# Two graph layers on one core: layer 1's linear part in 16 bits, its roots on GpSimd, and the copies re-dealt

## The chip, the core and the metric

The kernel runs on one core of a Trainium2 chip. The core has a matrix engine (TensorE, PE in the profile; its weight loads are PEld), three engines for element-wise work (VectorE or DVE, ScalarE or ACT, GpSimd or POOL), and SyncE (SP), which here only issues transfers. Each engine runs its own instructions in the order in which they were written, and waits where an operand or a buffer is not ready. PE writes to PSUM[...]. The metric is the time of one execution on the device in microseconds (us). Of the kernel before there are three runs: 272.62, 273.17 and 273.79, so the median is 273.17 us.

## What is computed

There are 4096 nodes with 64 features each, and a 0/1 adjacency matrix of 4096 x 4096 whose ones are rare (one in 256). Cut to what matters:

```python
# layer 0
mask = (adj != 0)
rank = cumsum(mask, axis=1)
deg  = rank[:, -1:]
k    = minimum(deg, 100)
pos  = rank - (deg - k)
w    = mask * where(pos > 0, 0.5 ** (k - pos), 0)      # the last neighbour weighs 1, the one before 1/2, ...
x    = layernorm(x + (w @ (x @ W0) + b0))
# layer 1
h    = (adj @ x + x) / (deg + 1)
out  = relu(concat([x, h]) @ W1 + b1)
out  = out / maximum(norm(out, axis=1), 1e-12)
x    = layernorm(x + out)
```

Layer 1 needs all rows of layer 0's result before any of its rows is complete, but sums over the rows that exist can begin early.

## The kernel before

**Tiles and steps.** The 4096 output rows are eight slabs `g` of 512 rows (R). The neighbours are eight groups `k` of 512, each of four blocks of 128 (KB = 4). Tile (g, k) of the transposed adjacency is 128 partitions x 4 x 512; it is loaded by POOL's queue from float32 into bf16 (512 KB in SBUF). The main loop has 64 steps, one for each tile: slab after slab, `k` from 7 down to 0, because a neighbour's weight depends on how many neighbours come after it. Step `i` is tile `steps[i]`.

**A step.** `count` (L237) adds up, on PE, how many ones each half block has; DVE turns this into the running count `cs` (L247, L249). `spread` (L255) makes from it, on PE, the number of later neighbours for every half block (`rep`), and ACT makes `near` of it (L257). `weigh` (L270, L280) adds on PE the place within the half block and the part from `near`; ACT (L287) and DVE (L288) each turn half of that into the 16 bits of the weight (`w`). `gather` (L298) multiplies the previous step's `w` with x, held as two fp16 parts side by side (`xhl`: high, and low times 2048), into `acc0`.

**Chunks.** `count` and `spread` do not run for one tile but for a chunk of them, and one chunk ahead: while a chunk is weighed, the tiles of the next one are counted. Slab 0 has chunks of one tile, slabs 1 to 3 of two, slabs 4 to 7 of four. A chunk of two has both tiles of the next one counted in its first step.

**Layer 0's end of a slab** is spread over the following steps by `at(i, engine, function)`: with i = 8(g+1), `first_hT` (ACT copies `acc0`, at i+1), `first_pz` (PE, W0 and the degree), `first_y`, `first_mv` (DVE, i+2), `first_s` (ACT, square root, i+3), `first_r`, `first_x1` (DVE, i+4), `first_hi`, `first_xl`, `first_lo` (the two fp16 parts `x1hl` of the new x, i+5 and i+6). Then x's part of layer 1: `first_px` (i+5) transposes x on PE in float32, `first_x1T` copies it to SBUF (ACT, i+6), and `first_pu` (PE, i+6) multiplies it, with a row of ones for b1, with both halves of W1 in float32 (L447). `first_c1` (DVE) adds the two results.

**Layer 1's sums** start in the loop: `some_sums` does up to four matmuls a step (L307) on the tiles of rows whose layer 0 is done (`ready`), and `evict_part` keeps sums of a part of the rows in SBUF.

**Buffers.** There are 23 bf16 tiles. Layer 1 needs every tile again, so the tiles of slabs 0 to 3 with k from 4 to 7 are copied to fp8 (`keep_next`, L320, one half tile a step from step 8 on, on ACT: 32 copies of 128 x 1024), which frees the bf16 tile for a later load. POOL issues one load a step, and stops at a load whose buffer is still read.

**The tail** is written out by hand. `own` completes each slab's sums, `last_hT` brings them to SBUF, `last_pz` multiplies with W1's lower half, `last_z` adds `c1`, `last_sq` and `last_ss` sum the squares, and `root_a` (ACT's square root) with `root_b` (four DVE instructions, L370 to L374) gives one over the norm. `last_y` scales (DVE) and adds x (POOL); `last_mv` takes mean and variance; root_a and root_b give one over the deviation; `last_o` scales and shifts, and the result is stored. This goes by units: slabs 5 and 2, then 0 and 1, then 4 and 3, then 6, then the halves 7a and 7b, each with roots of its own. On DVE, `last_hT` of slab 6 stands behind `last_y` of unit 4 and 3.

```python
n = 1 if g == 0 else 2 if g < 4 else 4
at(i + 5, PE, first_px, g)
at(i + 6, ACT, first_x1T, g)
at(i + 6, PE, first_pu, g)
return i >= NK * (k + 1) + 6 and i >= when[g, k]
```

## Time and profile before

| what | value |
|---|---|
| median of three runs | 273.17 us (272.62 to 273.79) |
| the profiled execution | 273.33 us |
| its span, first to last instruction | 271.5 us |
| mean granted TensorE clock | 0.965 |
| PE busy | 237.3 us (87%), 1865 instructions |
| DVE busy | 176.3 us (65%), 480 instructions |
| ACT busy | 157.9 us (58%), 226 instructions |
| POOL busy | 61.9 us (23%), 111 instructions |
| read from HBM | 69.34 MB |

A line of a group or of a timeline reads: start and duration in us (in a timeline), the engine, the line of the kernel, the operation, what it writes <- what it reads, the shape, how often. What stands in brackets is the time that the engine sat idle before it, and what ended that. The slices divide the span in 40 equal parts; a digit is the busy share in tenths, 9 is 90% or more. Busy shares are averages over stages that have different limits, so each stage is read by itself. Matmul ends are modelled; the distance from one start to the next is the better measure.

### The profile page before, as it was taken

To read this page: it belongs to the slowest core of one execution; us is meant where nothing else is said; L and a number is where in the kernel's file an instruction comes from. 1 tells how busy PE (TensorE), PEld (TensorE's weight loads), DVE (VectorE), ACT (ScalarE), POOL (GpSimd) and SP (SyncE) were. 2 spreads that over 40 slices of the span, in tenths; PEclk is the share of its full clock that TensorE was granted. 3 is DMA by queue.
4 is the path that set the end of the run, shared out by engine and by line. 5 is a ranking of instruction groups with operands and counts; after the bars stand their busy time and mean duration, and the time that the engine had idled before them with its cause. 6 is when DMAs were issued, how large, how long until landed. Compare 5 with 4: busy or idle time off the path is not lost.

```text
span 271.5 us, 4838 instructions
## 1 busy us (share of the span) xinstructions
PE 237.3 (87%) x1865; PEld 105.0 (39%) x1865; DVE 176.3 (65%) x480; ACT 157.9 (58%) x226; POOL 61.9 (23%) x111
## 2 busy tenths in 40 slices
PE   8397688979899999999899999999998999997820
PEld 2122124334434343443344344434343546555710
DVE  5566634875596778367846684576577456597884
ACT  4456627897798869768854463436545322146351
POOL 8565551231101320322122121210200000221100
PEclk9979959999999999999999999999999999999985
DMA  6999999999997999799999999990500000010010
GB/s 97 195 230 234 241 212 214 222 214 214 223 214 141 165 211 214 124 171 214 182 179 205 203 162 180 168 168 12 98 2 0 0 2 0 0 42 20 19 58 21
DMA packets 12072, 37.13 MB, mean 137 GB/s; under 512 B 2066, under 2 KB 3218, under 8 KB 12050
## 3 DMA queue, kind: packets, MB, share of 16 engines
q0 software_dynamic: 10128, 35.66, 68.1%
q1 hardware_dynamic: 1922, 1.18, 1.5%
q8 instruction: 14, 0.23, 0.3%
q14 instruction: 8, 0.07, 0.1%
HBM read 69.34 MB, written 1.05 MB: 259 GB/s over the span
## 4 chain that ended last, share of the span: by engine, by line
PE 51%; DVE 11%; ACT 8%; issue 3%; POOL 1%; DVEq 0%; POOLq 0%; ACTq 0%
PE acc L298 10%; PE acc_part L307 9%; PE v L270 8%; PE v L280 5%; ACT w L287 4%; PE acc_right L307 3%; DVE w L288 3%; PE cnt L237 3%; PE vb L307 3%; PE pu L447 2%; PE va L307 2%; PE pz L594 2%; PE pz L395 2%; DVE x L422 1%; ACT a L320 1%
## 5 line engine op out<-in xcount | busy, mean ns | idle before, releaser
L288 DVE TENSOR_SCALAR w<-v 128x1024 int16<-128x1024 f32 x64 | 78.2, 1222 | 45.3 <-PE v L280 45.2
L287 ACT ACTIVATE w<-v,less 128x1024 int16<-128x1024 f32 x64 | 71.3, 1114 | 56.9 <-PE v L280 39.9
L298 PE MATMUL acc<-w,xhl 128*128 128x512 bf16 x256 | 67.2, 385 | 2.4 <-ACT hT L389 2.1
L109 POOL DMA_DIRECT2D a<-in_adjT_dram x65 | 35.5, 548 | 122.1 <-PE acc_part L307 49.9
L270 PE MATMUL v<-a,tri 64*64 64x512 bf16 x512 | 42.0, 397 | 4.3 <-ACT w L287 2.6
L298 PEld LDWEIGHTS <-xhl 128*128 128x128 f16 x256 | 23.9, 99 | 32.5 <-issue 9.5
L320 ACT CAST a<-a 128x1024 fp8e4<-128x1024 bf16 x32 | 33.3, 1039 | 0.0
L307 PEld LDWEIGHTS <-x1hl 128*128 128x128 f16 x224 | 19.8, 98 | 27.0 <-issue 5.7
L307 PE MATMUL acc_part<-a,x1hl 128*128 128x512 bf16 x108 | 28.0, 381 | 1.8 <-ACT x1hl L434 1.3
L247 DVE TENSOR_TENSOR cs<-cnt,cs 128x512 bf16<-128x512 f32 x20 | 13.8, 691 | 20.5 <-PE cnt L237 20.4
L237 PE MATMUL cnt<-a,pick 128*32 128x512 bf16 x256 | 21.9, 399 | 6.0 <-DMA a<-in_adjT_dram 6.0
L280 PE MATMUL v<-near,mine 32*128 32x512 bf16 x256 | 25.7, 391 | 0.2 <-ACT near L257 0.2
L270 PEld LDWEIGHTS <-tri 64*64 64x64 bf16 x512 | 12.6, 106 | 30.2 <-issue 28.0
L257 ACT ACTIVATE near<-rep,most 128x512 bf16<-128x512 f32 x28 | 19.1, 682 | 3.8 <-PE rep L255 3.7
L633 POOL TENSOR_TENSOR y<-y,x 128x256 f32<-128x256 f32 x7 | 5.0, 726 | 56.1 <-DVE y L630 56.1
L280 PEld LDWEIGHTS <-mine 32*128 32x128 bf16 x256 | 6.5, 91 | 24.9 <-issue 24.9
L255 PE MATMUL rep<-cs,further 128*128 128x512 bf16 x28 | 11.2, 400 | 3.7 <-DVE cs L247 1.7
L307 PE MATMUL acc_right<-a,x1hl 128*128 128x512 fp8e4 (+1 forms) x56 | 12.7, 379 | 0.0
L237 PEld LDWEIGHTS <-pick 128*32 128x32 bf16 x256 | 4.6, 94 | 19.8 <-issue 11.5
L655 ACT ACTIVATE o<-y,off,r_l 128x64 f32<-128x64 f32 x28 | 9.7, 428 | 3.1 <-issue 1.7
L382 DVE BATCH_NORM_STATS2 st_l<-y 128x6 f32<-128x64 f32 x60 | 9.0, 214 | 0.7 <-POOL y L633 0.6
L427 ACT CAST x1hl<-x 128x256 f16<-128x256 f32 x8 | 3.2, 406 | 10.1 <-DVE x L422 10.1
(139 smaller groups left out, 238.6 us busy)
## 6 DMA issues: line engine op xcount, KB each, us to landing
a<-in_adjT_dram POOLq DMA_DIRECT2D x63, 512.0 KB, 9.7
c<-in_x_pairs_dram POOLq DMA_DIRECT2D x8, 128.0 KB, 11.6
x<-in_x_dram POOLq DMA_DIRECT2D x8, 128.0 KB, 7.9
out_dram<-o SPq DMA_DIRECT2D x7, 128.0 KB, 1.7
a<-in_adjT_dram POOLq DMA_DIRECT2D x2, 256.0 KB, 4.7
out_dram<-o_7a SPq DMA_DIRECT2D x1, 64.0 KB, 1.9
out_dram<-o_7b SPq DMA_DIRECT2D x1, 64.0 KB, 1.5
w_sb<-in_L_gnn_weight_dram SPq DMA_DIRECT2D x2, 16.0 KB, 6.5
```

Of the source, the lines that this page charges most:

```text
L109: nc.gpsimd.dma_start(out=a[:, qs, :], in_=adjT[g, k][:, qs, :])
L237: nc.tensor.matmul(cnt[g][q * 32 : (q + 1) * 32, :], lhsT=pick[:, PW - 2 * k : PW - 2 * k + 32], rhs=A[g][k][:, q, :], start=first, stop=last,
L247: nc.vector.tensor_tensor(new, cnt[g], cs[g], ALU.add)
L255: nc.tensor.matmul(pr, lhsT=further, rhs=cs[g], start=True, stop=True)
L257: nc.scalar.activation(near[g], pr, AF.Relu, bias=most, scale=-1.0)
L270: nc.tensor.matmul(v[i][halves[c], r, :], lhsT=tri[halves[r], :], rhs=A[g][k][halves[r], 2 * i + c, :], start=True, stop=False,)
L280: nc.tensor.matmul(v[i][:, r, :], lhsT=mine[rows, 2 * k : 2 * k + 2, :], rhs=nr[rows, :], start=False, stop=True,)
L287: nc.scalar.activation(w[:, 0:2, :], v[0], AF.Relu, bias=less)
L288: nc.vector.tensor_scalar(w[:, 2:4, :], v[1], -STEP * MAX_NEIGH, 0.0, ALU.add, ALU.max)
L298: nc.tensor.matmul(acc0[g], lhsT=xhl[:, b, :], rhs=w[:, q, :].bitcast(BF16), start=(k, q) == (NK - 1, 0), stop=(k, q) == (0, KB - 1),)
L307: nc.tensor.matmul(acc, lhsT=x1hl[:, b, :], rhs=A[g][b // KB][:, b % KB, :], start=first, stop=last)
L320: nc.scalar.copy(kept[g, k][:, qs, :], A[g][k][:, qs, :], saturate=False)
```

## The change

Seven things change.

1. Chunks of slab 1: four of one tile, then two of two; slabs 2 and 3 stay at four of two, slabs 4 to 7 at two of four.
2. `first_px` transposes `x1hl`, both fp16 parts at once, in fp16; `first_x1T` copies 128 x 512 instead of 64 x 512; `first_pu` is twelve matmuls with W1 in three bf16 parts (`w1_parts`, upper 64 partitions scaled by 1/2048) and one with ones and b1 in three bf16 parts. All three, and `ready`, come one step later. The parts are made on DVE in steps 7 and 8; W1 comes in four pieces and b1 for all partitions.
3. ACT's Sqrt runs once at the start, on a constant.
4. The fp8 copies skip steps that begin a slab, and start at step 9; in every fourth step DVE does one instead of ACT: 23 for ACT, 9 for DVE. They end at step 44 instead of 39.
5. `first_hT` is written right after the slab's last `gather`, ahead of the next copies.
6. In the tail, `root_p` on POOL (x to the power -0.5) takes the place of root_a and root_b for all norms but 7b's, and for the deviations of units 5 and 2, 0 and 1, and 6. Their offsets are made on POOL in two instructions.
7. The tail's order: slab 6's `last_hT` ahead of `last_y` of unit 4 and 3, slab 6's `last_pz` after a quarter of 7a's sums, outputs in pieces; 7a and 7b keep norms of their own but share one root for the deviation, one `last_o` and one store. 7a's x is added on POOL.

The diff, cut:

```diff
-        n = 1 if g == 0 else 2 if g < 4 else 4
-        chunks += [[(g, k) for k in range(k0, k0 - n, -1)] for k0 in range(NK - 1, -1, -n)]
+        sizes = {0: [1] * 8, 1: [1] * 4 + [2] * 2, 2: [2] * 4, 3: [2] * 4}.get(g, [4] * 2)
+        k = NK
+        for n in sizes:
+            chunks.append([(g, k - 1 - i) for i in range(n)])
+            k -= n
...
+    nc.scalar.activation(zero, zero, AF.Sqrt)
...
-    x1T = const.tile([D + 1, R], F32, name="x1T")
-    nc.vector.memset(x1T[D : D + 1, :], 1.0)
+    power = const.tile([P, 2 * TB], F32, name="power")
+    nc.vector.memset(power, -0.5)
+    x1T = const.tile([P, R], FP16, name="x1T")
+    ident16 = const.tile([P, P], FP16, name="ident16")
+    nc.vector.tensor_copy(ident16, ident)
...
+        for h in range(2):
+            for c in range(2):
+                nc.sync.dma_start(out=w1_sb[h * D : (h + 1) * D, c * D : (c + 1) * D], in_=w1[c * D : (c + 1) * D, :])
+        nc.sync.dma_start(out=b1_sb, in_=b1.partition_broadcast(P))
...
     def prepare_last():
         nc.vector.tensor_scalar(wn_sb[D:P, :], wn_sb[D:P, :], 1.0 / LO, None, ALU.mult)
+        nc.vector.tensor_scalar(w1_sb[D:P, :], w1_sb[D:P, :], 1.0 / LO, None, ALU.mult)
+        for j in range(3):
+            nc.vector.tensor_copy(w1_parts[:, j, :], w1_sb)
+            if j < 2:
+                nc.vector.tensor_tensor(w1_sb, w1_sb, w1_parts[:, j, :], ALU.subtract)
...
-        nc.scalar.copy(kept[g, k][:, qs, :], A[g][k][:, qs, :], saturate=False)
+        if i % 4 == 3:
+            nc.vector.tensor_copy(kept[g, k][:, qs, :], A[g][k][:, qs, :], saturate=False)
+        else:
+            nc.scalar.copy(kept[g, k][:, qs, :], A[g][k][:, qs, :], saturate=False)
...
-        return i >= NK * (k + 1) + 6 and i >= when[g, k]
+        return i >= NK * (k + 1) + 7 and i >= when[g, k]
...
+    def root_p(v, eps, name, tag):
+
+        n = v.shape[1]
+        r = small.tile([P, n], F32, tag=tag, name=f"{tag}_{name}")
+        if eps:
+            nc.gpsimd.tensor_scalar(r, v, eps, None, ALU.add)
+            v = r
+        nc.gpsimd.tensor_tensor(r, v, power[:, 0:n], ALU.pow)
+        return r
...
-        px = ep["px", g] = ps_m.tile([D, R], F32, tag="m", name=f"px_{g}")
+        px = ep["px", g] = ps_m.tile([P, R], FP16, tag="m", name=f"px_{g}")
         for t in range(TB):
-            nc.tensor.transpose(px[:, ts(t, P)], x1[:, g * TB + t, :], ident)
+            nc.tensor.transpose(px[:, ts(t, P)], x1hl[:, g * TB + t, :], ident16)
...
         for t in range(TB):
-            nc.tensor.matmul(pu[:, t, :], lhsT=x1T[:, ts(t, P)], rhs=w1_sb, start=True, stop=True)
+            for j in range(3):
+                nc.tensor.matmul(
+                    pu[:, t, :], lhsT=x1T[:, ts(t, P)], rhs=w1_parts[:, j, :], start=(t, j) == (0, 0), stop=False
+                )
+        nc.tensor.matmul(pu[:, :, 0:D], lhsT=ones.to_broadcast([P, P]), rhs=b1_parts, start=False, stop=True)
...
-    at(2 * NK + 2, DVE, prepare_last)
+    at(NK - 1, DVE, prepare_last)
+    at(NK, DVE, prepare_b1)
...
-        at(i + 1, ACT, first_hT, g)
...
-        at(i + 5, PE, first_px, g)
-        at(i + 6, ACT, first_x1T, g)
-        at(i + 6, PE, first_pu, g)
+        at(i + 6, PE, first_px, g)
+        at(i + 7, ACT, first_x1T, g)
+        at(i + 7, PE, first_pu, g)
...
-            if i >= NK:
-                keep_next()
+            if i > NK and i % NK:
+                keep_next(i)
             if held is not None:
                 gather(*held)
             held = (g, k, w)
+            if g > 0 and k == NK - 1:
+                first_hT(g - 1)
...
+    def last_rn(u, on_pool):
+        name, bs = u
+        ss = ep["ss", name]
+        if on_pool:
+            ep["rn", name] = root_p(ss, None, name, "rn")
+        else:
+            ep["rn", name] = root_b(root_a(ss, zero, f"n_{name}"), ss, zero, f"n_{name}")
...
+    def last_r(u, on_pool):
+        name, bs = u
+        v = ep["mv1", name][:, :, 1]
+        if on_pool:
+            ep["r1", name] = root_p(v, LN_EPS, name, "r1")
+            offset(u, nc.gpsimd)
+        else:
+            ep["r1", name] = root_b(ep["s1", name], v, eps_ln, f"l1_{name}")
+            offset(u, nc.vector)
...
     last_ss(u)
...
-    last_rn(u)
-    last_y(u, True)
+    last_rn(u, True)
     last_hT(6)
     acc[L, 0] = acc_of(L, "acc0", R // 2, "7a")
-    own_half(a_half, 0, NB // 2)
-    last_mv(u)
+    own_half(a_half, 0, NB // 4)
 
     v = unit(6)
     last_pz(v)
-    own_half(a_half, NB // 2, NB)
-    last_r(u, True)
+    own_half(a_half, NB // 4, NB)
+    last_y(u, True)
     last_z(v)
     last_sq(v, False)
     last_ss(v)
+    last_rn(v, True)
     half_hT(a_half)
...
+    last_y(wb, False, y[:, 2:4, :])
+    last_mv(wb, mv[:, 2:4, :])
+    last_s(w)
+    last_r(w, False)
+    last_o(w, 0, 2)
+    last_o(w, 2, 4, on_act=False)
+    store(w)
```

## The prediction

> **What bounds the kernel now.** I read the page's slices first, then the stretches by engine, then the orders of time of TensorE (PE), GpSimd (POOL) and VectorE (DVE), then the waits. The slices:
>
> ```profile
> PE   8397688979899999999899999999998999997820
> PEclk9979959999999999999999999999999999999985
> DMA  6999999999997999799999999990500000010010
> ```
>
> Each digit is 6.8 us. Until about 70 us the DMA is full and PE has holes. From 70 to 245 us PE is the bound. In the last 25 us neither is: a chain over the small engines ends the run. Two early stretches and two of the loop (PE, PEld, DVE, ScalarE (ACT), POOL busy; PE clock; DMA):
>
> ```profile
> 33.00:36.00 3.00, 1.16 (x12) 0.29 (x11) 0.49 (x1) 0.00 (x0) 3.00 (x6) 0.66 1.06 213
> 36.00:39.00 3.00, 3.00 (x17) 0.68 (x9) 1.72 (x3) 1.69 (x2) 1.13 (x3) 0.50 1.03 208
> 90.00:113.00 23.00, 21.99 (x196) 9.54 (x193) 16.68 (x37) 19.05 (x24) 4.07 (x8) 1.00 1.03 192
> 163.00:188.00 25.00, 24.42 (x209) 10.25 (x208) 15.80 (x35) 11.86 (x15) 3.43 (x6) 1.00 0.79 142
> ```
>
> PE had work for 1.16 of the 3 us before 36, and then ran at half its clock (0.50), always busy. In the loop ACT is 83% busy while it makes fp8 copies, 47% after. PE's holes, in order of time, and one POOL line:
>
> ```profile
> 34.84 0.62 PE L237 MATMUL cnt<-a,pick 128*32 128x512 bf16 x4 [2.68 <-DMA a<-in_adjT_dram]
> 44.76 1.02 PE L298 MATMUL acc<-w,xhl 128*128 128x512 bf16 x4 [1.05 <-ACT hT L389]
> 55.46 0.63 PE L270 MATMUL v<-a,tri 64*64 64x512 bf16 x8 [1.42 <-ACT w L287]
> ...
> 52.46 0.72 POOL L227 TENSOR_TENSOR x<-x,b_sb 128x256 f32<-128x256 f32 x1 [7.02 <-DMA x<-in_x_dram]
> ```
>
> The POOL line dates the DMA: tile (1,6) came at 34.84, seven tiles and one x block later is 52.46, so 2.43 us a tile. The waits (total, times, longest):
>
> ```profile
> PE v L270 <- ACT w L287: 2.6, 5, 1.4
> PE acc L298 <- ACT hT L389: 2.1, 2, 1.0
> PE acc_part L307 <- ACT x1hl L434: 1.3, 3, 0.5
> PE rep L255 <- ACT x1T L442: 0.9, 1, 0.9
> ```
>
> The end, PE then DVE:
>
> ```profile
> 250.59 1.10 PE L594 MATMUL pz<-wn_sb,hT 128*128 128x64 f32 x8 [1.39 <-DVE hT L566]
> 256.29 0.66 PE L594 MATMUL pz_7a<-wn_sb,hT 128*128 128x64 f32 x4 [1.10 <-ACT hT L573]
> 260.36 0.66 PE L594 MATMUL pz_7b<-wn_sb,hT 128*128 128x64 f32 x4 [1.66 <-ACT hT L573]
> ...
> 261.86 0.28 DVE L601 TENSOR_TENSOR z_7b<-pz_7b,c 128x128 f32<-128x128 f32 x1
> 268.09 0.54 DVE L659 TENSOR_SCALAR o_7b<-y_7b,mv_l_7b,r_l_7b 128x64 f32<-128x64 f32 x2
> ```
>
> PE waits 4.15 us for three hT copies; DVE then works 6.77 us alone, and the store and end take 2.9.
>
> **The skill.** The Trainium skill, "TensorE: Matmul & The Clock Gate", Part 1, says that an idle window of about 3.4 us halves the PE clock; here 2.68 us without work sufficed. "GPSIMD Engine Reference", section 3, gives 2.6 cycles an element for two inputs (555 ns for 256); the trace has 0.73 us for 128x256, so some 0.17 us is fixed. Its section 8 says that POOL shares SBUF interfaces with DVE operations of two SBUF inputs; the trace agrees: sq_7a took 0.81 us beside a POOL add, sq_7b 0.29 alone.
>
> **Early part.** Before, slab 1 is in chunks of two, so step 7 counts two tiles at once and starves. That cost 2.68 us, and the work from 34.84 to 41.44 took 6.6 us where the same groups, summed from later rows, take 3.8: 2.8 more. With the waits of 1.05, 1.42 and 0.3 that is 8.2 us before step 16's count at 64.33. After, slab 1's first four chunks are single. But the tiles are the floor: step 12 counts (1,0), which lands at 34.84+6x2.43 = 49.4; step 14 counts (2,6), 54.9. SyncE issues ten weight DMAs instead of eight: two more pieces of W1 and b1 for all partitions, some 256 packets more. The hardware queue's 1922 packets are 1.5% of 271.5 us, so the tiles come up to 0.5 us later. The last weights are issued 1.1 us later and land, 10 us after that, near 24 us; step 7 wants them at 33, so that is hidden. On DVE, step 7 gains seven instructions (near rows 0.19 to 0.29, sum 1.6 us) and step 8 seven more (1.45). Queued behind them on DVE is the next cs; rep on PE waits for cs, and gather stands behind rep: PE loses 0.9 and then 1.0. hT now leads the copies (1.05 gone), and the Sqrt table is loaded at the start where ACT waits for ident, so the load of 1.28 us at 51.87, behind the 1.42, is gone. I worked the steps through with the rows' durations, each engine in its order: step 12's count at 50.0 (was 51.23), step 14's at 55.4 (57.75), step 16's at 61.9. So of the 8.2 us most only turn into shorter waits for tiles. **-2.4** (0 to -3.5). Two more rep, near and cs (0.22, 0.68, 0.69) are inside. No hole exceeds 1.1 us, so I keep the full clock.
>
> **PE work.** Per slab: px was 0.44 us (159.03 to 159.46), pu 0.89. After, px is four fp16 transposes, pu twelve matmuls of 128 columns and one of 256. The trace has no stream of 128-column 16-bit matmuls. The clock-gate page, "Back-to-back issue gap", gives 56 ns alone, 81 with weight loads; in the trace four loads with one column take 0.17 us and 256 columns 0.108 each, weight load hidden, so I take 60: px 0.24, pu 0.72+0.11. Saving 0.25, slabs 1 to 7: **-1.75** (at 56 -2.3, at 81 +0.5). Slab 0 is in the early part.
>
> **Loop waits.** Of 6.9 us that PE waits for ACT in the four rows, 2.8 was early; 4.1 remains. ACT loses 9 of 32 copies (9x1.04 = 9.4 us), x1T moves to the step after lo, ready() starts layer-1 sums a step later, which is what x1hl held up. I take 3.2 gone. DVE gets nine copies: the trace has 0.68 us for 1024 columns in SBUF (mine); "VectorE: DVE Perf Modes", the tier table, allows that rate for copies; at one a cycle it is 1.2. That is 6 to 11 us on a DVE 65% busy, but each copy can stand ahead of a cs: 1.0 back. **-2.2** (+1 to -4).
>
> **DMA.** Copies now skip steps 8, 16, and so on, 7 in 8 steps, and so free their tiles one to two steps later (a slab 3 copy done at step 37 is now at 39, and feeds a tile counted at step 42). POOL's load waits for that copy, and all later loads and x blocks stand behind it in POOL's queue; PE's count is what waits for them. Two to three steps of 3 us are left between the issue and the count. A lone tile with its x block took 5.5 us (issued 190.90, x there 196.4); a pair takes 2.43 more. So the prefetch hides the delay barely, and without it each late pair would cost 1 to 3 us: **+0.7** (0 to +3).
>
> **Tail.** POOL, idle in the tail but for adds, gets eight roots, three offsets (two instructions each) and the add of y_7a; ACT loses its square roots for them, DVE four to five small instructions each (0.16 to 0.23). POOL pow is in no row. Low bound: an add, 0.17 + 8x0.0022 = 0.2 us; high, 100 times the element price, 2 us. I take 0.7 for 8 columns, near the geometric middle; ACT and DVE together now take 1.25 (247.97 to 249.22). While a root is late, the y behind it on DVE waits, and all that DVE has after that. Up to the end of slab 6's sums at 247.3 PE's own work covers this: y_5_2 stands behind hT_1, 2.3 us after its sum of squares, and hT_3 comes in time even with roots of 2 us. Then hT_6 no longer queues behind y_4_3: DVE is free at 247.8, hT_6 done 248.5 (was 250.54). pz of slab 6 starts at 248.55, 24 half matmuls of 0.108 end 7a at 252.0, 7b's first half hides 7a's hT, 7b ends 255.95, pz_7b starts 256.55: 3.8 earlier. DVE between 248.5 and 257.2: y_4_3 0.69, slab 6 to max 1.45, moments 1.85, y_6 0.42, root and offset 1.0, 7a to max 1.1, slab 6's moments 0.96, y_7a 0.29: 7.8 of 8.7, so it fits, with 0.9 to spare. On POOL the add of y_7a stands behind slab 6's root and offset (0.9 us from 256.75), and 7a's moments on DVE wait for it; ready at 258.1, DVE asks at 258.3. The final DVE run loses 7a's own root and offset (five, 1.0 us) but 7b's waits for ACT's two square roots stay: about 6.1 from 257.2. Last o at 263.3, was 268.63: 5.3. Port sharing as at sq_7a, 0.7: **-4.6** (-1.5 to -6).
>
> **Sum.** -2.4-1.75-2.2+0.7-4.6 = -10.25. The profiled execution took 273.33 us with a span of 271.5; span 261.25, time 263.1. The median, 273.17, gives **262.9, say 263.0**.
>
> **Rivals.** (1) Only the ends gain: DVE and late tiles take the loop's place as fast as ACT leaves it (+3 on DMA and loop waits, PE at 81 ns). For it: 9 copies on an engine in every step; against: 4.1 us of ACT waits in the rows. 273.2-2.4-4.6+2 = 268. 20%. (2) Everything in the loop goes: 258, from the good ends of loop and PE. 12%. (3) Slower: POOL's roots. Four of them (8, 4, 2, 4 columns) lie in series in the last chain, 2.25 times the 8-column price, and four 8-column ones between 230 and 248. From about 2.5 us each those run over, and at 3.8 the 2.25x3.1 = 7 and some 3 us of overrun eat all 10 us; at 5, about 277. Against: the two-input rate is ordinary; for: pow is unmeasured. 4%. (4) The starved gap only moves to step 12 and halves the clock again: +2.8, 265.8, inside the main case. No change at all would need gains cancelling: 3%.
>
> **Chances.** Main case 61%, 259.5 to 266.5. Range 259 to 268.5, leaving out half of (2), the upper end of (1), (3). This kernel's runs spread 0.4%, so 0.5% is what can be told from none. Faster 0.93, same 0.03, slower 0.04.
>
> **What would show it.** No table load near 52 us; no wait of over 1.5 us on count at step 7 and clock 1.0 at 36 to 39; pu no longer than 0.89 per slab; ACT under 150 us; hT_6 before y_4_3; one root for slab 7. Wrong if POOL's pow exceeds 2 us, if count waits for DMA after 70 us, or if rep waits for cs in every slab.

## The result

The changed kernel takes 266.06 us (median of four runs, 265.07 to 267.25), the kernel before 273.13 (272.62 to 273.79) in the same comparison. The ratio is 0.974, with a 95% interval of 0.970 to 0.979: 7.1 us faster, where the forecast was 10.25. 266.06 lies inside the range of 259.0 to 268.5 and 3 us above the likeliest value. The profiled execution took 266.06 us with a span of 264.2, so 1.86 us lie outside the span (1.83 before).

The page of the changed kernel, the slices of PE, its clock and the DMA (one digit is 6.6 us):

```profile
PE   8499868889989997999899999999997989999930
...
PEclk9659999999999999999999999999999999999975
DMA  6999999999999999699799999996500000000111
```

The clock no longer falls in the sixth slice; in this trace it is lower in the second and third instead (0.6 and 0.5, where before had 0.9 and 0.7), to which the last section comes back. The DMA is still full up to 105 us, then has a slice of 0.6 (106 to 112 us) and one of 0.7 (125 to 132). The last 20 us still belong to the small engines. The same four stretches as before (PE, PEld, DVE, ACT, POOL busy; PE clock; DMA):

```profile
33.00:36.00 3.00, 2.36 (x25) 0.68 (x21) 2.25 (x4) 1.93 (x3) 2.67 (x5) 1.00 1.06 212
36.00:39.00 3.00, 1.48 (x16) 0.56 (x16) 2.83 (x9) 1.23 (x2) 1.87 (x4) 1.00 1.06 213
90.00:113.00 23.00, 21.58 (x201) 8.88 (x199) 15.98 (x36) 15.20 (x20) 5.07 (x8) 1.00 0.93 168
163.00:188.00 25.00, 24.35 (x215) 10.01 (x215) 15.72 (x34) 12.15 (x15) 4.48 (x8) 1.00 0.83 154
```

PE has work for 2.36 us before 36 instead of 1.16, and clock 1.00 behind it. But PE is busy only 21.58 of 23 us in the stretch where ACT used to be the trouble, less than before (21.99), while ACT's share there fell from 83% to 66%. The holes of PE, in order of time, say why:

```profile
38.41 0.38 PE L284 MATMUL rep<-cs,further 128*128 128x512 bf16 x1 [1.52 <-DVE cs L276]
...
41.92 0.38 PE L284 MATMUL rep<-cs,further 128*128 128x512 bf16 x1 [1.06 <-DVE cs L276]
...
55.59 0.40 PE L266 MATMUL cnt<-a,pick 128*32 128x512 bf16 x4 [0.47 <-DMA a<-in_adjT_dram]
...
62.28 0.61 PE L266 MATMUL cnt<-a,pick 128*32 128x512 bf16 x8
```

```profile
104.74 0.40 PE L266 MATMUL cnt<-a,pick 128*32 128x512 bf16 x4 [1.36 <-DMA a<-in_adjT_dram]
...
135.65 0.40 PE L266 MATMUL cnt<-a,pick 128*32 128x512 bf16 x4 [0.24 <-DMA a<-in_adjT_dram]
```

```profile
210.26 1.03 PE L336 MATMUL va<-a,x1hl 128*128 128x512 bf16 x4
...
217.41 0.40 PE L482 MATMUL px<-ident,x1hl 128*128 128x128 f16 x4 [0.78 <-ACT x1hl L477]
...
244.80 1.10 PE L646 MATMUL pz<-wn_sb,hT 128*128 128x64 f32 x8 [0.30 <-DVE hT L618]
...
252.94 0.66 PE L646 MATMUL pz_7b<-wn_sb,hT 128*128 128x64 f32 x4 [0.52 <-ACT hT L625]
```

In steps 7 and 8, rep waits for cs, 1.52 and 1.06 us. Later one tile is late by 1.36 us at 104.74. In the tail px waits 0.78 for the low part of `x1hl`; of the three waits for hT that the prediction shows, one is gone, and the others fell from 1.39 to 0.30 and from 1.66 to 0.52. POOL's new rows, by shape:

```profile
L416 POOL TENSOR_TENSOR rn<-ss,power 128x8 f32<-128x8 f32 x3 | 5.0, 1668 | 35.8 <-DVE ss L670 35.8
...
L416 POOL TENSOR_TENSOR r<-r,power 128x4 f32<-128x4 f32 x1 | 1.0, 1037 | 0.1
L416 POOL TENSOR_TENSOR rn<-ss,power 128x4 f32<-128x4 f32 x1 | 1.0, 1017 | 0.1
L416 POOL TENSOR_TENSOR rn_7a<-ss_7a,power 128x2 f32<-128x2 f32 x1 | 0.7, 706 | 1.8 <-DVE st_l L425 1.8
```

A root of eight columns takes 1.67 us, of four 1.02 to 1.04, of two 0.71: about 0.16 us a column on top of 0.4. And the last chain on DVE:

```profile
253.90 0.28 DVE L653 TENSOR_TENSOR z_7b<-pz_7b,c 128x128 f32<-128x128 f32 x1
...
256.26 0.35 DVE L425 BATCH_NORM_STATS2 st_l_7a<-y 128x6 f32<-128x64 f32 x2 [1.23 <-POOL y L690]
...
260.25 0.54 DVE L732 TENSOR_SCALAR o<-y,mv,r_l 128x64 f32<-128x64 f32 x2
```

DVE waits 1.23 us for POOL's add of y_7a. It stands on POOL behind slab 6's root and offset (253.75 to 255.81).

**Where the 7.3 us of span came from.** Three points on PE divide the run:

| stretch | before | after | gained | forecast |
|---|---|---|---|---|
| start to step 16's count | 64.33 | 62.28 | 2.05 | 2.4 |
| from there to the tail's first sums | 150.28 (to 214.61) | 147.98 (to 210.26) | 2.3 | 3.0 |
| from there to the end of the span | 56.9 (to 271.5) | 53.94 (to 264.2) | 2.95 | 4.85 |

The forecast column puts -1.75 for PE's work as 1.5 (six slabs) in the loop and 0.25 (slab 7) in the tail. All three stretches gained, each less than forecast.

### The profile page after: what moved, and what is told of

Same layout as the page of the kernel before. It is cut to its first block, busy times and chain, and to the rows that moved or that the text cites. A ratio compares the mean times of both kernels' runs of the same rounds, so it can differ in the third digit from the quotient of the medians.

```text
span 264.2 us, 4902 instructions
## 1 busy us (share of the span) xinstructions
PE 234.4 (89%) x1907; PEld 102.4 (39%) x1907; DVE 178.7 (68%) x465; ACT 147.9 (56%) x210; POOL 77.4 (29%) x129
## 3 DMA queue, kind: packets, MB, share of 16 engines
q1 hardware_dynamic: 2080, 1.25, 1.7%
HBM read 69.40 MB, written 1.05 MB: 267 GB/s over the span
## 4 chain that ended last, share of the span: by engine, by line
PE 39%; DMA 23%; DVE 14%; issue 10%; POOL 7%; ACT 5%; POOLq 0%; ACTq 0%; DVEq 0%
DMA a<-in_adjT_dram 18%; PE v L299 7%; PE acc L327 6%; PE acc_part L336 6%; DMA c<-in_x_pairs_dram 5%; DVE w L317 4%; PE v L309 4%; ACT w L316 3%; PE acc_right L336 3%; POOL a L112 3%; PE cnt L266 2%; PE pz L646 2%; PE va L336 2%; DVE x L465 2%; PE vb L336 2%
## 5 line engine op out<-in xcount | busy, mean ns | idle before, releaser
L316 ACT ACTIVATE w<-v,less 128x1024 int16<-128x1024 f32 x64 | 71.3, 1114 | 56.9 <-PE v L309 32.5
L112 POOL DMA_DIRECT2D a<-in_adjT_dram x65 | 37.1, 573 | 116.4 <-PE acc_part L336 40.1
L266 PE MATMUL cnt<-a,pick 128*32 128x512 bf16 x256 | 22.8, 396 | 7.0 <-DMA a<-in_adjT_dram 6.2
L276 DVE TENSOR_TENSOR cs<-cnt,cs 128x512 bf16<-128x512 f32 x22 | 15.1, 688 | 16.6 <-PE cnt L266 16.5
L352 ACT CAST a<-a 128x1024 fp8e4<-128x1024 bf16 x23 | 23.9, 1038 | 0.0
L286 ACT ACTIVATE near<-rep,most 128x512 bf16<-128x512 f32 x30 | 20.5, 682 | 5.1 <-PE rep L284 5.0
L284 PE MATMUL rep<-cs,further 128*128 128x512 bf16 x30 | 12.0, 398 | 5.2 <-DVE cs L276 4.2
L416 POOL TENSOR_TENSOR rn<-ss,power 128x8 f32<-128x8 f32 (+1 forms) x4 | 6.0, 1505 | 35.9 <-DVE ss L670 35.8
L266 PEld LDWEIGHTS <-pick 128*32 128x32 bf16 x256 | 5.3, 94 | 22.4 <-issue 14.3
L660 ACT ACTIVATE sq<-z 128x512 f32<-128x512 f32 x3 | 1.9, 630 | 17.2 <-DVE z L653 17.2
L256 POOL TENSOR_TENSOR x<-x,b_sb 128x256 f32<-128x256 f32 x8 | 5.9, 735 | 11.4 <-DMA x<-in_x_dram 11.3
```

Source lines behind the costliest of these rows:

```text
L112: nc.gpsimd.dma_start(out=a[:, qs, :], in_=adjT[g, k][:, qs, :])
L266: nc.tensor.matmul(cnt[g][q * 32 : (q + 1) * 32, :], lhsT=pick[:, PW - 2 * k : PW - 2 * k + 32], rhs=A[g][k][:, q, :], start=first, stop=last,
L276: nc.vector.tensor_tensor(new, cnt[g], cs[g], ALU.add)
L284: nc.tensor.matmul(pr, lhsT=further, rhs=cs[g], start=True, stop=True)
L286: nc.scalar.activation(near[g], pr, AF.Relu, bias=most, scale=-1.0)
L316: nc.scalar.activation(w[:, 0:2, :], v[0], AF.Relu, bias=less)
```

## Experiments

Each kernel below is the changed kernel with the one edit shown. Those run together share their runs of the kernel before, whose medians were 273.19, 272.98 and 273.18. The changed kernel's own interval is 1.2 us to either side. So a difference of half a microsecond in the medians decides nothing, and I read it from the traces: by stretches, each from its own start. A trace is one execution, though. The five kernels that have the changed tail as it is took 53.89 to 53.97 us for it in their traces. So an execution's span less the tail of its kernel's trace gives an estimate of when its tail began, without a trace of it. Seven kernels here, the changed one among them, are the same up to slab 7's px: over their 33 executions the estimate has a median of 210.2 us (31 of them 209.1 to 210.9, two later). This is the mark for the loop below.

| run | median (us) | ratio to before, 95% interval |
|---|---|---|
| changed kernel | 266.06 | 0.974 (0.970 to 0.979) |
| slab 1 in pairs | 266.32 | 0.976 (0.974 to 0.979) |
| px and pu in float32 | 266.47 | 0.976 (0.974 to 0.977) |
| a copy in every step, ahead of hT | 265.20 | 0.971 (0.970 to 0.973) |
| y_7a's add first on POOL | 265.46 | 0.973 (0.971 to 0.976) |
| px later in the tail | 264.46 | 0.968 (0.966 to 0.970) |
| W1's and b1's parts made later | 267.48 | 0.981 (0.978 to 0.985) |
| old tail | 269.41 | 0.986 (0.984 to 0.988) |
| one more root on POOL | 267.21 | 0.980 (0.976 to 0.984) |
| a copy behind hT | 264.30 | 0.968 (0.966 to 0.970) |
| y_7a's add on DVE | 265.28 | 0.972 (0.970 to 0.974) |
| three mends together | 262.36 | 0.961 (0.960 to 0.963) |
| roots back on ACT and DVE | 267.11 | 0.978 (0.976 to 0.980) |

### The early part: chunks, and the tiles behind them

```diff
-        sizes = {0: [1] * 8, 1: [1] * 4 + [2] * 2, 2: [2] * 4, 3: [2] * 4}.get(g, [4] * 2)
+        sizes = {0: [1] * 8, 1: [2] * 4, 2: [2] * 4, 3: [2] * 4}.get(g, [4] * 2)
```

> The changed kernel with slab 1's chunks put back to four of two tiles; all else as changed. The profile of the changed kernel has step 16's count at 62.28 us, 2.05 earlier than before. Theory (the chunks make the early gain): step 7 again counts two tiles at once, PE waits for the second one for over 1.5 us, and the count of step 16 comes 1.5 to 2.1 later: 267.6 to 268.2 us. Rival (the early gain comes from hT ahead of the copies and from the table load at the start, and the tiles' arrival is the floor whatever the chunks): step 16's count moves by under 0.5, 266.1 to 266.6 us.

Measured: 266.32. PE with slab 1 in pairs:

```profile
35.46 0.62 PE L266 MATMUL cnt<-a,pick 128*32 128x512 bf16 x4 [2.73 <-DMA a<-in_adjT_dram]
...
62.77 0.61 PE L266 MATMUL cnt<-a,pick 128*32 128x512 bf16 x8
```

The starved wait is back in full, 2.73 us, and the clock behind it is 0.50 (36 to 39 us), after less idle time than the 3.4 us window of the Trainium skill's "TensorE: Matmul & The Clock Gate", Part 1, as in the kernel before; yet step 16's count is only 0.49 later, and at 104.86 PE waits for the same tile as at 104.74. The rival holds, though only just: it had said under 0.5. With the rest of the change in place, the most visible hole of the kernel before is worth half a microsecond. The other 1.56 us of the early gain are there with pairs too: its counts run 0.5 ahead of before at 46 to 51 us, where before lost 1.05 at hT, and 2.1 ahead at 55.62, past the place where before waited 1.42 for ACT's w behind the table load. (0.5 of these 2.1 is px, which before had done by then and which now comes a step later.) That these two edits make it is read from the two traces; no run had them alone.

### PE's work in 16 bits

```diff
-            nc.tensor.transpose(px[:, ts(t, P)], x1hl[:, g * TB + t, :], ident16)
+            nc.tensor.transpose(px[:, ts(t, P)], x1[:, g * TB + t, :], ident)
...
-            for j in range(3):
-                nc.tensor.matmul(
-                    pu[:, t, :], lhsT=x1T[:, ts(t, P)], rhs=w1_parts[:, j, :], start=(t, j) == (0, 0), stop=False
-                )
-        nc.tensor.matmul(pu[:, :, 0:D], lhsT=ones.to_broadcast([P, P]), rhs=b1_parts, start=False, stop=True)
+            nc.tensor.matmul(pu[:, t, :], lhsT=x1T[:, ts(t, P)], rhs=w1_f, start=True, stop=True)
```

> The changed kernel with px and pu back in float32 (x1 transposed in float32, four float32 matmuls with a row of ones for b1), at the changed kernel's steps. The bf16 parts are still made on DVE in steps 7 and 8 and used by nothing, so that only PE's part differs; three more small weight transfers. Theory (0.25 us of PE a slab, seven slabs on the path): +1.75, less up to 0.78 in the tail, because a float32 px does not wait for the low part of x1hl: 267.0 to 267.8 us. Rival (in the loop PE's saving is eaten by later waits, as PE reaches DMA and DVE earlier): under +0.5, at most 266.6 us, with the saved time standing as longer waits on count and v in the changed kernel.

`w1_f` holds both halves of W1 and the row of b1 in float32. Measured: 266.47, the rival's number, but not by the rival's mechanism. PE with float32 px and pu:

```profile
104.30 0.40 PE L271 MATMUL cnt<-a,pick 128*32 128x512 bf16 x4 [0.65 <-DMA a<-in_adjT_dram]
...
135.91 0.40 PE L271 MATMUL cnt<-a,pick 128*32 128x512 bf16 x4 [0.24 <-DMA a<-in_adjT_dram]
```

```profile
211.12 1.03 PE L341 MATMUL va<-a,x1hl 128*128 128x512 bf16 x4
...
217.32 0.60 PE L487 MATMUL px<-ident,x 128*64 128x128 f32 x4
...
220.35 1.06 PE L497 MATMUL pu<-w_f,x1T 65*128 65x128 f32 x8
```

In the tail of the changed kernel px is 0.23 us from start to start (217.41 to 217.64) and pu 0.78 (220.23 to 221.01); in that of before they are 0.55 and 0.90 (219.94, 223.94 to 224.84). So in the tail 16 bits save PE 0.3 to 0.4 a slab. In the loop, from the start of px and of pu to the start of what follows each, they save between 0.14 and 0.32 in slabs 1 to 6 and 1.45 in sum, against 1.5 forecast: the price was right.

How much of this arrives at the tail? In this trace the float32 kernel is 0.86 late at the tail's first sums (211.12), which looks as if late tiles had swallowed the rest. But PE's wait at 104.30 is shorter than the changed kernel's mainly because the tile itself came 0.44 earlier, and the loads ahead of it were issued 0.28 later (96.65 against 96.37): this execution had a quick transfer. By the four executions its tail began between 211.1 and 212.0 us, in the middle 1.3 behind the mark of 210.2, of 1.6 that the float32 work costs up to there (slab 0 included). So most of it goes through. Then the tail gives 0.63 back up to pz_7b (253.17 in the trace, 0.23 behind the changed kernel's 252.94), because a float32 px reads x1 and does not wait for the low part. That is what brings the median so near to the changed kernel's: 16 bits gain in the loop, and the wait that comes with them takes about half of it back.

### The late tile in the loop

```diff
-            if i > NK and i % NK:
+            if i >= NK:
                 keep_next(i)
```

> The changed kernel with the fp8 copies in every step from step 8 on, those that begin a slab too; still every fourth on DVE. Theory (the skipped steps make the tiles late: PE waits 1.36 us for a tile at 104.74 and 0.24 at 135.65): copies end at step 39, these two waits go, and ACT has a copy beside hT again, which stands ahead of it: -1.0 to -1.6 unless a wait on w comes back, so 264.5 to 265.6 us. Rival (those tiles are late because the transfers queue one behind another, not because of the copies): the waits for tiles stay over 1 us, and ACT's extra copy costs 0 to +1: 266.0 to 267.0 us.

```diff
             if g > 0 and k == NK - 1:
                 first_hT(g - 1)
+                keep_next(i)
```

> The changed kernel with an fp8 copy in the steps that begin a slab too, from step 16 on, but written behind the slab's hT instead of ahead of it. The run with a copy in every step lost the waits for tiles at 104.74 and 135.65 (1.36 and 0.24 us) and had a wait of 1.04 for hT at 66.72 instead; its first sums of the tail came 1.05 us earlier. Theory (the later copies are what makes the tiles late, and the wait for hT is separate): both kinds of wait are gone, the first sums of the tail come 1.0 to 1.8 earlier, 264.3 to 265.1 us. Rival (the tile at about 104 us is bound by the stream itself): a wait for it of over 0.6 us stays, 265.4 to 266.2 us.

Measured: 265.20 with a copy in every step ahead of hT, 264.30 with it behind hT (this kernel has a copy in step 8 too, at 40.13). PE with the copy ahead, then with it behind:

```profile
66.72 1.02 PE L327 MATMUL acc<-w,xhl 128*128 128x512 bf16 x3 [1.04 <-ACT hT L432]
...
103.17 1.05 PE L266 MATMUL cnt<-a,pick 128*32 128x512 bf16 x16
```

```profile
102.47 1.05 PE L266 MATMUL cnt<-a,pick 128*32 128x512 bf16 x16
...
109.80 0.61 PE L266 MATMUL cnt<-a,pick 128*32 128x512 bf16 x8
```

Neither has a wait for a tile at 104 or 135 any longer (the sixteen matmuls that count four tiles run on without a break, from 103.17 and from 102.47); in the first, the wait for hT at 66.72 came back. The tail's first sums are 1.05 and 1.73 us earlier than in the changed kernel (209.21 and 208.53 against 210.26); by all executions it is 1.0 and 1.8 ahead of the mark. So the copies that the change skips are what made the tiles late: a copy frees a buffer that POOL's next load waits for. In the changed kernel's waits (total, times, longest) that is POOL's own row:

```profile
POOL a L112 <- ACT a L352: 28.9, 9, 6.6
```

The spread agrees. In the traces of the seven kernels with the same loop the tile at 104 came between 103.95 and 105.06, and their tails began between 209.48 and 210.60, 1.1 us apart. With the copy behind hT all four runs lie within 0.24 us.

### Making the parts later

```diff
-    at(NK - 1, DVE, prepare_last)
-    at(NK, DVE, prepare_b1)
+    at(NK + 3, DVE, prepare_last)
+    at(NK + 5, DVE, prepare_b1)
```

> The changed kernel with the making of W1's parts moved from step 7 to step 11 and of b1's from step 8 to step 13 on DVE, where the profile has DVE less in demand; pu of slab 0 reads them in step 15. In the changed kernel rep waits 1.52 and 1.06 us for cs in steps 7 and 8, behind these instructions. Theory (up to about 135 us the arrival of the tiles is the floor, so a wait in front of it costs nothing): rep's waits fall under 0.3 each, the waits for tiles in steps 12 and 14 grow, step 16's count comes at most 0.5 earlier, and the time is 265.6 to 266.2 us. Rival (these waits are lost time): step 16's count comes 1 to 2.5 earlier and the time is 263.6 to 265.0 us.

Measured: 267.48, slower than either theory had it. PE with the parts made later:

```profile
50.22 0.40 PE L266 MATMUL cnt<-a,pick 128*32 128x512 bf16 x4 [2.06 <-DMA a<-in_adjT_dram]
...
55.51 0.40 PE L266 MATMUL cnt<-a,pick 128*32 128x512 bf16 x4 [0.50 <-DMA a<-in_adjT_dram]
...
58.74 0.38 PE L284 MATMUL rep<-cs,further 128*128 128x512 bf16 x1 [1.35 <-DVE cs L278]
...
63.63 0.61 PE L266 MATMUL cnt<-a,pick 128*32 128x512 bf16 x8
```

Half of the theory holds: without the two waits of 2.58 us PE is at step 12 two microseconds early (its first count at 47.76 instead of 49.73), and waits 2.06 there for the tile that comes at 50.22, where it came at 50.33. The waits in steps 7 and 8 cost nothing. But my new place was not free: behind the tile of step 14 (55.51 and 55.59) there is no further tile to wait for up to step 16, and b1's seven instructions, then in front of cs, hold rep up for 1.35 us, which stays in step 16's count (63.63 against 62.28). It stays to the end: by five of the six executions the tail began between 211.1 and 212.5, and the median of all is some 1.4 behind the mark. (The traced one, 270.38 us, was the slowest; it lost more behind the tile at 104, which came at 106.68, and is read here only ahead of it.)

Why is the tile at 50 a floor, and the one at 104 not? The loads say it. From 31 to 54 us POOL issues them at the same times within 0.25 us in this kernel, in the one with pairs and in the changed one, though PE is up to two microseconds early or late in between: there the transfers set the pace. From 60 us on a load waits for a buffer that PE's sums or ACT's copies set free, and so it moves with the steps. A load ahead of the tile at 104, in the changed kernel and with the parts made later:

```profile
96.37 0.53 POOL L112 DMA_DIRECT2D a<-in_adjT_dram  x1 [1.34 <-ACT a L352]
```

```profile
97.71 0.53 POOL L112 DMA_DIRECT2D a<-in_adjT_dram  x1 [1.34 <-ACT a L352]
```

It is issued 1.34 later, as late as the step itself. So the same instructions cost nothing ahead of a tile whose arrival does not depend on PE, and all of their time where the next tile's load waits for the steps.

### The tail as a whole, and its roots

The first kernel has everything behind `first_c1(L)` as before the change (its diff is the change's own, of that part, turned round). The second keeps the new order and has the roots on ACT and DVE: `last_sn` and `last_s` are the square root on ACT, `last_rn` and `last_r` then four instructions on DVE where the result is wanted, and the outputs of units 0 and 1 stand behind the root of 4 and 3. Its edit, for one unit:

```diff
-    last_rn(u, True)
+    last_sn(u)
...
+    last_rn(u, False)
...
-    last_r(u, True)
+    last_s(u)
...
+    last_r(u, False)
```

> The changed kernel with everything behind slab 7's first_c1 as in the kernel before: its order, its roots on ACT and DVE, slab 7's halves each with roots and a store of their own. Slab 7's px and pu stay in 16 bits. This is the worth of parts 6 and 7 together. Theory (the profile of the changed kernel: the tail from its first sums to the end lost 2.95 us, of which 0.25 are PE's saving for slab 7 and 0.78 a new wait of px that stays here): +3.2 to +3.6, 269.2 to 269.7 us. Rival (the forecast's 4.6): 270.4 to 270.9 us. Second rival (PE's earlier sums are taken back by the final chain on DVE in any case): +1.5 or less, at most 267.6 us.

> The changed kernel's tail in its new order, with the roots of layer 1 back on ACT (square root) and DVE (four instructions, and a fifth for the offset) instead of POOL; each square root is written where ACT is free, outputs of units 0 and 1 behind the root of 4 and 3; POOL keeps the adds. This parts the worth of the roots' place from that of the order, which together are 3.35 us. Theory (DVE sets the end from slab 6's hT on: four roots and an offset there are 3.4 us more for DVE, and its two waits for POOL of 1.18 and 1.23 go): +0.6 to +1.5, 266.7 to 267.6 us. Rival (a POOL root of 1.67 us is no gain, the order is all): 265.5 to 266.2 us. Second rival (ACT's and DVE's turns back and forth are the cost, as before the change): +2.5 or more, over 268.5 us.

Measured: 269.41 with the old tail and 267.11 with the roots back, both as the first theory had it. From the tail's first sums to the end of the span the old tail takes 57.29 us (210.41 to 267.7), the roots on ACT and DVE 54.7 (210.60 to 265.3), the changed kernel 53.94. So the order, with slab 7's shared root and the outputs in pieces, is worth 2.6 us and the roots' place, given this order, 0.8. The old order with roots on POOL was not run. DVE with the roots back, the last root before slab 7's second half and that half:

```profile
254.06 0.13 DVE L402 TENSOR_TENSOR q_n_7a<-s_n_7a 128x2 f32<-128x2 f32 x1
...
255.28 0.16 DVE L402 TENSOR_TENSOR q_l<-s_l 128x4 f32<-128x4 f32 x1
...
256.23 0.16 DVE L706 SCALAR_TENSOR_TENSOR off<-mv_l,r_l 128x4 f32<-128x4 f32 x1
256.31 0.28 DVE L653 TENSOR_TENSOR z_7b<-pz_7b,c 128x128 f32<-128x128 f32 x1
...
260.35 0.16 DVE L402 TENSOR_TENSOR q_l<-s_l 128x4 f32<-128x4 f32 x1 [0.42 <-ACT s_l L396]
```

The profile shows no wait of DVE from 254.06 to 256.31, and z_7b, whose input pz_7b (from 253.47, 0.66 us) is done at about 254.1, starts at 256.31. In the changed kernel it starts at 253.90. Of these 2.4 us some come back, as DVE's wait of 1.23 for y_7a is gone; 0.8 are left at the end. A POOL root of 1.67 us is longer than ACT's and DVE's 1.25 together, and still a gain, because here DVE is the engine that runs out of time.

### The new wait of px

```diff
-    own(0, 16, 20)
+    own(0, 16, 24)
     first_px(L)
     first_x1T(L)
-    own(0, 20, 24)
```

> The changed kernel with slab 7's px put four matmuls later, behind slab 0's sums up to block 24 instead of block 20. In the changed kernel PE waits 0.78 us at 217.41 for the low part of x1hl, which the float32 px of before did not read. Theory (PE is the bound of the tail up to the half sums of slab 7, so a wait of PE goes to the end): the wait goes and everything behind it comes 0.7 to 0.8 earlier, 265.2 to 265.5 us. Rival (the roots on POOL and DVE's order set the tail, so PE only waits later): 265.8 to 266.2 us.

Measured: 264.46. The wait is gone, and the tail takes 53.12 us (209.48 to 262.6) instead of 53.94: 0.82, the theory's size. The other 0.8 of the difference in medians lies ahead of the tail, where the two kernels are the same: it is the spread of the tile at 104 (103.96 here) and not this edit's.

### The final chain, and POOL's drain

```diff
-    last_r(v, True)
     y = ep["y1", w[0]] = epi.tile([P, TB, D], F32, tag="near", name="y1_7")
     mv = ep["mv1", w[0]] = small.tile([P, TB, 2], F32, tag="mv", name="mv_7")
     last_y(wa, True, y[:, 0:2, :])
+    last_r(v, True)
```

> The changed kernel with slab 6's root and offset on POOL written behind the add of y_7a instead of ahead of it. In the changed kernel DVE waits 1.23 us at 256.26 for this add, which stands behind a root of 1.04 us and three more instructions on POOL. Theory (this wait is on the chain that ends the run): DVE's moments of 7a start right after 7b's maximum, and the last output comes 0.7 to 1.2 earlier: 264.9 to 265.4 us. Rival (slab 6's outputs, now about 0.7 us later on ACT, hold up ACT's square root for 7a and 7b, and the gain is given back): 265.8 to 266.3 us.

Measured: 265.46. DVE's wait is gone, and the last output, counted from the tail's first sums, ends 0.96 us earlier (49.94 us behind them instead of 50.90). But the tail to the end of the span is 53.81 instead of 53.94, so all but 0.13 is given back; the median, which is nearer to the theory's number, has the spread ahead of the tail in it. The gain is given back as the rival had it, but not for its reason: ACT's root, and with it the last output, did come earlier. The rows of the drain instructions at the program's end, on POOL's and SP's queues (how many, then their shortest, median and longest duration in ns, then the start in us of the first and the last), for the changed kernel and then for this one:

```profile
L903 POOLq DRAIN  x3: 46/102/7317, 255.6 to 263.9; - x3
L903 SPq DRAIN  x3: 7/7/7, 263.3 to 263.6; - x3
```

```profile
L903 POOLq DRAIN  x3: 46/93/6984, 255.8 to 263.3; - x3
L903 SPq DRAIN  x3: 7/7/13, 261.8 to 263.0; - x3
```

At the program's end the last drains of all five queues start within 0.3 us (263.6 to 263.9 in the changed kernel); this is the last barrier, at which the engines wait for one another. POOL's long drain has to be the first of its three, as no 7 us are left behind the start of the last one. POOL's drain lasts 7.317 us from 255.6, to about 262.95, 6.7 after the end of POOL's last instruction (256.23); here it lasts 6.984 from 255.8, to 262.8, again 6.7 after the last one (256.07). SP, done with the stores, reaches its own first drain at 263.3 in the changed kernel, and at 261.8 here. So here the stores are done, and the barrier waits for POOL. One more root on POOL tests that alone:

```diff
     last_y(wa, True, y[:, 0:2, :])
+    extra = small.tile([P, 2 * TB], F32, tag="rn", name="extra")
+    nc.gpsimd.tensor_tensor(extra, least[:, 0 : 2 * TB], power, ALU.pow)
```

> The changed kernel with one more root of 8 columns on POOL (1.67 us in the profile) behind POOL's last instruction; nothing reads it, no output changes. In the changed kernel POOL's last add ends at 256.23, then POOL is in a final drain of 7.3 us, until about 263.4; the last store has landed at about 262.8, and the last barrier starts near 263.3. Theory (the end waits for POOL's drain as well as for the last store, and the two are nearly level): the last output stays where it is and the end comes 1.6 to 1.9 later, 267.6 to 268.0 us. Rival (the drain only spans the time in which POOL has nothing to do, and ends with the stores): no change, 265.8 to 266.3 us.

```profile
L905 POOLq DRAIN  x3: 46/102/8907, 255.6 to 265.0; - x3
L905 SPq DRAIN  x3: 7/7/7, 263.3 to 264.7; - x3
```

Measured: 267.21, between the two numbers. SP is at its drain at 263.3 as before, POOL's drain now ends at 264.5, 6.7 after 257.78, and the span ends 1.1 later. The theory's mechanism is shown. Its size was wrong, because I took the two paths as level, while POOL was 0.35 ahead (I had counted the 7.3 us from POOL's last add, but the row starts at 255.6). The drain costs the changed kernel nothing, but anything that shortens its final chain by more than 0.35 us has to end POOL's work earlier too. This edit does both:

```diff
-    last_y(wa, True, y[:, 0:2, :])
+    last_y(wa, False, y[:, 0:2, :])
```

> The changed kernel with the add of y_7a on DVE (0.29 us by the row of 7b's) instead of POOL; slab 6's root stays on POOL, now as POOL's last work. DVE's wait of 1.23 us for POOL at 256.26 is gone, and POOL's last instruction ends about 0.4 earlier than with the changed kernel. In the runs so far POOL's final drain ended 6.7 us after its last instruction: 264.9 before, 262.95 in the changed kernel, 262.8 with y_7a's add first, 264.5 with one more root. Theory (the last output and the drain both bound the end): the last output comes 0.8 to 1.0 earlier than in the changed kernel, counted from the tail's first sums, the drain ends level with the last store, and the end comes 0.7 to 1.0 earlier: 265.0 to 265.4 us. Rival (the drain holds the end as with y_7a's add first): 0.2 or less, 265.8 to 266.1 us.

Measured: 265.28. The drains:

```profile
L903 POOLq DRAIN  x3: 46/93/6982, 255.0 to 262.5; - x3
L903 SPq DRAIN  x3: 7/7/7, 261.8 to 262.2; - x3
```

The tail takes 53.08 us (209.72 to 262.8), 0.86 less; the drain ends at 262.0 and SP's drain starts at 261.8. They are level, as the theory had it.

### Together

> The changed kernel with three mends together: a copy behind hT in the steps that begin a slab, px four matmuls later in the tail, and the add of y_7a on DVE. Theory (they lie at different places of one path: PE in the loop, PE in the tail, DVE in the final chain): 1.0 to 1.8 and 0.8 and 0.7 to 1.0 add up to 2.5 to 3.6, 262.5 to 263.6 us. Rival (the mend in the loop is taken back by tiles or by DVE's w): 1.5, 264.5 us.

Measured: 262.36, ratio 0.961 (0.960 to 0.963), faster than both kernels: 3.7 us below the changed kernel and 10.8 below the one before. It is 0.14 below the theory's range, less than the changed kernel's own interval. The loop gives 1.92 (tail's first sums at 208.34), the tail 1.78 (52.16 us). Here the drain is what is last:

```profile
L903 POOLq DRAIN  x3: 46/102/6982, 252.8 to 260.2; - x3
L903 SPq DRAIN  x3: 7/7/7, 259.5 to 260.0; - x3
```

POOL's long drain ends at 259.8, 0.3 behind the start of SP's. By this trace a shorter final chain alone would gain nothing more.

## The prediction, point by point

**Early part, forecast 2.4, measured 2.05.** The steps came where the working put them: step 12's count with its second tile at 50.33 (50.0 forecast), step 14's at 55.59 (55.4), step 16's at 62.28 (61.9). The waits for cs, forecast 0.9 and 1.0, were 1.52 and 1.06, and were free. "The tiles are the floor" was right and stronger than I used it: the chunks that the working began with are worth 0.5 of the 2.05, and the rest was there without them. So the number came nearly true with a first cause that did little.

**PE work, forecast 1.75; 1.45 saved in slabs 1 to 6, and a new wait of px in slab 7.** The price was right: twelve matmuls in 0.67 us are 56 ns each, where I took 60; the 81 ns that the Trainium skill's "TensorE: Matmul & The Clock Gate", "Back-to-back issue gap", gives for pairs of weight load and 128 columns did not occur. px is 0.23 in the tail. By the executions with float32 most of the loop's part goes through. The step that failed is slab 7: there the forecast had another 0.25, and px's wait of 0.78 turned it into a loss of 0.63. So undoing all of part 2 on PE moved the median by only 0.4.

**Loop, forecast 3.0, measured 2.3: waits 2.2, DMA 0.7.** PE's waits for ACT and DVE between step 16 and the tail were 5.78 us before, 3.93 of them up to 151.16. Of these 1.29 are left in the changed kernel (up to 135): 2.64 gone, more than forecast. Behind 151 they grew, from 1.85 to 2.34, most of it the last wait for DVE's w (0.70 before, 1.13 at 204.49). So 2.15 went on balance, as forecast. Which of the parts took them (fewer copies on ACT, hT ahead of the copies, the later x1T) was not run apart, except for hT: with a copy ahead of it, its wait of 1.04 is back. DVE made a copy in 0.68 us, the lower of the two prices that the forecast weighed. The step that failed in the loop is the term for the tiles, which was mis-sized: 0.7 forecast, 1.36 and 0.24 measured, so 1.6, inside its bounds of 0 to 3. This 0.9 is more than all that the loop lacks (2.15 less 1.6 is 0.55; the other 1.75 of the 2.3 are work, most of it px and pu). The prediction called the loop PE-bound from 70 us on, but its own line for 90 to 113 us has the DMA at 1.03, and in the slices the DMA stays at 9, with two slices of 7, up to 183 us, which left a late load little room to catch up. The mechanism, that skipped copies free their tiles later and POOL's queue stands behind them, is shown by the two runs that put copies back.

**Tail, forecast 4.6 and 0.25 for PE, measured 2.95.** The order of events came as forecast: hT of slab 6 ahead of y_4_3, 7a's hT hidden, one root for slab 7. Of the missing 1.9, 1.3 arise before z_7b. The wait of px, 0.78, was not in the sum: I priced the transposes and missed that an fp16 px reads what the float32 one did not. The other 0.5 are small pieces; the largest is 0.3 at z_7b, where DVE, which I had with 0.9 to spare, was not free: POOL's root had held y_4_3 up for 1.18. From z_7b to the last output I had 6.1, and 0.7 for shared ports over the whole stretch; it took 7.26 (to 261.16, on ACT), so 0.46 more, and 0.14 are at the very end. The step that failed behind z_7b is y_7a's add: forecast ready 0.2 before DVE asks, it came 1.23 after. The mis-sized term behind both is the root on POOL: 0.7 us for eight columns, measured 1.67, and slab 6's root and offset held POOL until 255.81.

**The rivals.** The first, that only the ends gain, names the right place for part of it: late tiles took 1.6 us of the loop's gain, but not all. The second did not come. The third, POOL's roots as a loss, was wrong in sign: at 1.67 us the roots on POOL are a gain of 0.8 against ACT and DVE. The fourth, a starved gap at step 12, did not come. Of the signs listed, the absent table load, the clock of 1.00 at 36 to 39, pu at 0.78, ACT at 147.9 us and hT of slab 6 at 244.07 all agree; of the signs that would make it wrong, count waits for the DMA after 70 us did show, and that was the miss in the loop.

## What to carry to other kernels

What a wait ahead of a late transfer is worth depends on what starts the transfer. If the stream of transfers runs on by itself, what is saved ahead of it is waited away, and what is lost there is free. If the transfer waits for a buffer that the steps set free, it moves with them, and savings and delays ahead of it count. One trace can mislead here: a transfer that was quick by chance looks like a saving that was lost. When an operand changes its form, look at who makes the new one and when; a cheaper instruction can wait for more. A slower engine can still be the right place for small work if the faster one sets the end, but then its own last instruction must be in time too.

## What was not expected

- POOL's final drain ended 6.7 us after POOL's last instruction in every trace where I followed it (before 264.9 after 258.20; 262.95 after 256.23; 262.8 after 256.07; 264.5 after 257.78; 262.0 after 255.29), and the end of the program waits for it where it comes last.
- POOL's power of a few columns costs far more a column than its adds: 1.67, 1.03 and 0.71 us for eight, four and two columns, where an offset's product of eight columns takes 0.20.
- The PE clock between 10 and 20 us stood anywhere from 0.51 to 0.83 in traces of kernels that hardly differ there, and the count at about 35.5 us moved by no more than 0.54 with it: there, too, PE waits for tiles.
- In the traced execution with the parts made later, a wait of 1.97 us for the tile at 106.68 was followed by a clock of 0.50 (108 to 110 us), while one of 2.06 us at 50.22 was not (1.00 from 50 to 57): the length of the last wait alone does not tell.
